# Expert slots of two sizes in a two-layer attention and mixture-of-experts kernel

## The chip, the core and the metric

The kernel runs on one core of one Trainium2 chip. The metric is the device time of one launch in microseconds (us), here the median of several runs. Everything is in fp32.

## What is computed

The input is x of shape (8, 256, 32, 32): 8 batches of 1024 tokens with 256 channels. The reference, cut to what matters:

```
x = attention(x, w_qkv, w_out) + x          # layer 0: 8 heads of 64, softmax over the queries
t = tokens(x)                               # (8, 1024, 256)
n = layer_norm(t)
t = t + softmax((n @ W.T) @ n.T) @ n        # layer 1: one head of 256
n = layer_norm(t)
probs = softmax(n @ router_w.T)             # 8 experts
rw, re = top_k(probs, 2); rw = rw / sum(rw) # two experts for each token
t = t + n + sum over e of combine[:, e] * (gelu(n @ w1[e] + b1[e]) @ w2[e] + b2[e])
```

Every expert has two 256 x 256 matrices. A token goes to 2 of the 8 experts, so batches 0 to 6, with 7168 tokens, give 14336 rows of expert work.

## The kernel before

The batches go one after the other through layer 0 (`layer0`), the attention of layer 1 (`attend`) and the router. The experts of batches 0 to 6 are not computed in their own batch. Each batch's normalized tokens are scattered by `dispatch` into a table in HBM, `rows`: expert e owns the rows from e x 7168 on, its tokens stand there in order, and each row carries two more numbers, the gate and the place of its result. The table is zeroed at the start; past an expert's last row there are zeros. In batch 7 the experts of the seven batches are run over the table as one stage, between the output projection of layer 0 (line 734) and the attention of layer 1. The experts of batch 7 itself come at the end, over all tokens (`dense`), and there the results of the stage are added to batches 0 to 6 (`Results`).

The stage works in slots. A slot is 256 rows (`BR`) of one expert. The number of slots is fixed when the kernel is built: 14336 / 256 + 7 = 63, enough for any split of the rows over 8 experts. Which rows and which weights a slot takes is worked out on the chip by `plan`, a generator on VectorE that is advanced three times during layer 0 of batch 7, beside the projections of head pairs (`project_pair`, line 402): its first half counts blocks for each expert and puts them in an order in which experts of the lower and the upper half alternate; its second half turns each slot's block into a first row and offsets of weights and biases (`row_at`, `w_at`, `b1_at`, `b2_at`). Slots without a block point at zero rows beyond the table, whose targets are out of bounds, so nothing is written for them.

For slot b the function `experts` does:
- `fetch`: four DMAs on the SP queue bring the rows as four squares of channels into `xr` (4 buffers), a fifth the gates and targets into `where`
- `stage`: ScalarE copies the slot's weights into `w_ring` (4 buffers, line 1348)
- `turned`: VectorE transposes `xr` into `xb` (line 1375)
- `hidden`: 4 matmuls `ph` (line 1386, weights stationary, the slot's rows as columns), then 2 gelus on ScalarE (line 1398)
- `collect`: for each 128 rows 2 matmuls `pe` with 256 columns (line 1415), then VectorE adds the bias into `yb` (2 buffers, line 1425)
- `send`: VectorE scales by the gate (line 1440) and forms the targets (line 1443), and GpSimd scatters each 128 rows into `y` in HBM with an indirect DMA (line 1447)

The loop runs these over different slots at once: in one turn `hidden` of b-3, `stage` of b-1, `fetch` of b, `turned` of b-2, `collect` of b-4. An `issue_after` puts an instruction behind another on its queue without a wait. Into turns of the loop small steps of batch 7's layer norm are put. The last four slots (`LATE`) are finished inside the attention of layer 1 of batch 7, as filling.

Of the kernel before, what the change touches and what calls it, by code (L numbers as in the profile page):

```python
# [10 lines left out]
F32 = mybir.dt.float32  # L11
I32 = mybir.dt.int32
# [7 lines left out]
def kernel(  # L20
# [45 lines left out]
    RUN = BR // SQ  # L66
# [96 lines left out]
    for e in range(E):  # L163
# [10 lines left out]
    )  # L174
    HALVES = (NBMAX + 1) // 2
    half_iota = const.tile([P, HALVES, 2], F32, name="half_iota")
    nc.gpsimd.iota(
        half_iota,
        [[1, HALVES], [0, 2]],
        base=0,  # L180
        channel_multiplier=0,
        allow_small_or_imprecise_dtypes=True,
    )
    odd_iota = const.tile([P, HALVES, 2], F32, name="odd_iota")
    nc.gpsimd.iota(
        odd_iota,
        [[0, HALVES], [1, 2]],
        base=0,
        channel_multiplier=0,
        allow_small_or_imprecise_dtypes=True,  # L190
# [885 lines left out]
    class Group:  # L1076


        def __init__(self, n, items):
            self.n, self.items = n, items  # L1080
            self.cap = len(items) * S
            self.nb = 2 * self.cap // BR + E - 1
            self.rows = dram.tile([E * self.cap + BR, DW], F32, name=f"rows_{n}")
            self.views = dram_disjoint_views(self.rows, 2 * NT * len(items))
            self.sums = [dram.tile([P, NT, D], F32, name=f"sums_{b}") for b in items]
            self.y = dram.tile([2 * self.cap, D], F32, name=f"y_{n}")
            self.ways = dram_disjoint_views(self.y, R * self.nb)
            self.counts = None
            self.planes = self.y.rearrange("(k n p i) d -> n p k i d", k=2, p=P, i=NT)
# [118 lines left out]
    def plan(group):  # L1208


        n, nb, cap = group.n, group.nb, group.cap
        counts = group.counts
        steps = cap // BR

        def tmp(tag, shape, dtype=F32):
            return small.tile([P, *shape], dtype, tag=tag, name=f"{tag}_{n}", bufs=1)


        below = tmp("p_below", [E, steps])
        edge = tmp("p_edge", [steps])  # L1220
        nc.vector.tensor_scalar_mul(edge, b_iota[:, :steps], float(BR))
        nc.vector.tensor_tensor(
            below,
            counts.unsqueeze(2).to_broadcast([P, E, steps]),
            edge.unsqueeze(1).to_broadcast([P, E, steps]),
            ALU.is_gt,
        )
        blocks = tmp("p_blocks", [E])
        nc.vector.tensor_reduce(blocks, below, AX.X, ALU.add)
        ends = tmp("p_ends", [E])  # L1230
        nc.vector.tensor_tensor_scan(ends, ones[:, :E], blocks, 0.0, ALU.mult, ALU.add)
        first = tmp("p_first", [E])
        nc.vector.tensor_sub(first, ends, blocks)

        left = ends[:, E // 2 - 1 : E // 2]
        right = tmp("p_right", [1])
        nc.vector.tensor_sub(right, ends[:, E - 1 : E], left)
        turns = tmp("p_turns", [1])
        nc.vector.tensor_tensor(turns, left, right, ALU.min)
        rest = tmp("p_rest", [1])  # L1240
        nc.vector.tensor_tensor(rest, right, left, ALU.is_gt)
        nc.vector.tensor_mul(rest, rest, left)
        nc.vector.tensor_sub(rest, rest, turns)
        twice = tmp("p_twice", [1])
        nc.vector.tensor_add(twice, turns, turns)
        block = tmp("p_block", [nb])
        after = tmp("p_after", [nb])
        taking = tmp("p_taking", [nb])
        half = half_iota.rearrange("p h t -> p (h t)")[:, :nb]
        odd = odd_iota.rearrange("p h t -> p (h t)")[:, :nb]  # L1250
        nc.vector.scalar_tensor_tensor(block, odd, left, half, ALU.mult, ALU.add)
        nc.vector.tensor_scalar_add(after, b_iota[:, :nb], rest)
        nc.vector.tensor_scalar(taking, b_iota[:, :nb], twice, None, ALU.is_lt)
        nc.vector.tensor_sub(block, block, after)
        nc.vector.tensor_mul(block, block, taking)
        nc.vector.tensor_add(block, block, after)
        unused = tmp("p_unused", [nb])
        nc.vector.tensor_scalar(
            unused, b_iota[:, :nb], ends[:, E - 1 : E], float(nb), ALU.is_ge, ALU.mult
        )  # L1260
        nc.vector.tensor_add(block, block, unused)
        base = tmp("p_base", [E])
        nc.vector.tensor_scalar_mul(base, first, -float(BR))
        yield

        mine = tmp("p_mine", [nb, E])
        of = block.unsqueeze(2).to_broadcast([P, nb, E])
        nc.vector.tensor_tensor(
            mine, of, ends.unsqueeze(1).to_broadcast([P, nb, E]), ALU.is_ge
        )  # L1270
        e_of = tmp("p_e", [nb])
        nc.vector.tensor_reduce(e_of, mine, AX.X, ALU.add)
        nc.vector.tensor_tensor(
            mine,
            e_of.unsqueeze(2).to_broadcast([P, nb, E]),
            e_iota.unsqueeze(1).to_broadcast([P, nb, E]),
            ALU.is_equal,
        )

        work = tmp("p_work", [nb, E])  # L1280
        lo, hi = tmp("p_lo", [nb]), tmp("p_hi", [nb])
        nc.vector.tensor_mul(work, mine, base.unsqueeze(1).to_broadcast([P, nb, E]))
        nc.vector.tensor_reduce(lo, work, AX.X, ALU.add)
        nc.vector.scalar_tensor_tensor(lo, block, float(BR), lo, ALU.mult, ALU.add)
        nc.vector.scalar_tensor_tensor(lo, e_of, E - 0.5, lo, ALU.is_lt, ALU.mult)
        nc.vector.scalar_tensor_tensor(lo, e_of, float(cap), lo, ALU.mult, ALU.add)
        nc.vector.tensor_scalar_min(e_of, e_of, float(E - 1))
        row_at = keep.tile([P, NBMAX], I32, tag="row_at", name=f"row_at_{n}", bufs=1)
        placed = nc.vector.tensor_copy(row_at[:, :nb], lo)
        where = [row_at]  # L1290
        for what, each in (("w", WE), ("b1", NFC), ("b2", D)):
            nc.vector.tensor_scalar_mul(hi, e_of, float(each))
            at = keep.tile([P, NBMAX], I32, tag=f"{what}_at", name=f"{what}_at_{n}", bufs=1)
            with tc.issue_after(placed.ins):
                placed = nc.vector.tensor_copy(at[:, :nb], hi)
            where.append(at)
        group.where = where
        yield placed

    def experts(group, behind, table, steps):  # L1300
# [55 lines left out]
        def fetch(b):  # L1356
            xr = rowp.tile([P, RUN, DQ], F32, tag="xr", name=f"xr_{n}_{b}")
            with tc.issue_after((loads[-1] if loads else evicted["relayed"]).ins):
                at = register(b, 0)
            mine = group.rows[bass.ds(at, BR), :D].rearrange("(s t) (k d) -> k t s d", s=RUN, k=NQ)  # L1360
            for k in range(NQ):
                loads.append(nc.sync.dma_start(xr[ts(k, SQ)], mine[k]))
            where = small.tile([P, R, 2], F32, tag="where", name=f"where_{n}_{b}", bufs=8)
            loads.append(
                nc.sync.dma_start(
                    where, group.rows[bass.ds(at, BR), D:].rearrange("(r p) c -> p r c", r=R)
# [5 lines left out]
        def turned(b, xr):  # L1372
            xb = two.tile([P, NCC, BR], F32, tag="xb", name=f"xb_{n}_{b}")
            with tc.issue_after(behind.ins):
                squares = nc.vector.transpose(  # L1375
                    xb.rearrange("p cc (s t) -> p s cc t", t=SQ),
                    xr.rearrange("p s (cc c) -> p s cc c", c=SQ),
                )
            return xb, squares

        def hidden(b, xb):
            wb = firsts.pop(b)
            ph = big(f"ph_{n}_{b}")
            for fc in range(NFC):
                for dc in range(NCC):
                    last = nc.tensor.matmul(  # L1386
                        ph[:, ts(fc, BR)],
# [6 lines left out]
            hT = two.tile([P, NFC, BR], F32, tag=f"qk{1 if late else b % 2}", name=f"hb_{n}_{b}")  # L1394
            at = register(b, 2)
            for fc in range(NFC):
# [3 lines left out]
                        ph[:, ts(fc, BR)],  # L1400
# [7 lines left out]
        def collect(b, hT, last, squares):  # L1408
            wb = seconds.pop(b)
            py = acc(f"pe_{n}_{b}")  # L1410
            at = NCC * FF
            with tc.issue_after(last.ins) if last else nullcontext():
                for r in range(R):
# [8 lines left out]
            yb = two.tile([P, R, D], F32, tag="yb", name=f"yb_{n}_{b}")  # L1422

            def add():
                return nc.vector.tensor_add(
                    yb,
                    py.rearrange("p (r d) -> p r d", d=D),
                    b2_flat[:, bass.ds(register(b, 3), D)].unsqueeze(1).to_broadcast([P, R, D]),
# [8 lines left out]
        def send(b, yb):  # L1437
            if True:
                where = wheres.pop(b)
                scaled = nc.vector.tensor_mul(yb, yb, where[:, :, 0:1].to_broadcast([P, R, D]))  # L1440
                evicted["scaled"] = scaled
                to = small.tile([P, R], I32, tag="to", name=f"to_{n}_{b}", bufs=4)
                nc.vector.tensor_scalar(
                    to, where[:, :, 1], -1.0, float(2 * group.cap), ALU.mult, ALU.add
                )
            for r in range(R):
                sent = nc.gpsimd.indirect_dma_start(  # L1447
                    out=group.ways[R * b + r][:, :],
# [329 lines left out]
```

## Time and profile before

| | us |
|---|---|
| median of 3 runs | 2275.53 |
| lowest and highest run | 2273.93 and 2275.75 |
| profiled execution, its own time | 2280.71 |
| its span, first to last instruction | 2279.0 |
| first `ph` matmul of the expert stage | at 1857.8 |
| last `ph` matmul of the loop | at 2066.3 |

The profile is of one execution on the chip. Times of rows are from the start of its span. An engine's row in the timeline reads: start, duration, engine, line, operation, output and inputs, number of instructions, and in brackets the idle time before it and what ended it. PE is TensorE's matmuls, PEld its weight loads, DVE VectorE, ACT ScalarE, POOL GpSimd, SPq the DMA queue of SyncE. One fp32 matmul shows as two records, each with a weight load.

### The profile page before, as it was taken

What the parts mean: (1) busy time and instruction counts of PE and PEld (TensorE: products, weight loads), DVE (VectorE), ACT (ScalarE), POOL (GpSimd) and SP (SyncE); (2) the same over time, 40 slices, a digit from 0 to 9 for tenths busy, and PEclk for the clock granted to TensorE, in tenths of its full rate; (3) what the DMA queues carried; (4) which work ended last, traced back from release to release, by engine and by line L of the source; (5) the groups of instructions that cost most, each with busy time, mean ns of one, the idle gap of its engine ahead of it and who ended that gap; (6) DMA issues with size and microseconds to landing.
All of it is one profiled execution on the core that took longest, in us unless ns stands there. A gap on an engine that the chain in (4) does not pass through costs nothing.

```text
span 2279.0 us, 38069 instructions
## 1 busy us (share of the span) xinstructions
PE 2239.6 (98%) x13061; PEld 1209.0 (53%) x13061; DVE 1567.8 (69%) x3923; ACT 1232.1 (54%) x2221; POOL 316.3 (14%) x321
## 2 busy tenths in 40 slices
PE   9999999999999999999999999999999999999998
PEld 3345534563356335643555345534563378885666
DVE  5775678567865787577756775678567957555667
ACT  3664566356636564746564664566356645555411
POOL 1000012000300030002000120012000315552100
PEclk9999999999999999999999999999999999999999
DMA  8996201020102010201011000200041136662486
GB/s 281 359 354 191 52 15 43 4 60 8 50 1 46 19 52 6 39 26 45 13 22 43 31 27 13 52 15 25 5 90 51 51 71 150 146 146 53 124 259 170
DMA packets 278265, 182.82 MB, mean 80 GB/s; under 512 B 196676, under 2 KB 233335, under 8 KB 277048
## 3 DMA queue, kind: packets, MB, share of 16 engines
q1 hardware_dynamic: 264808, 150.08, 24.5%
q0 software_dynamic: 11632, 29.78, 3.7%
q8 instruction: 104, 1.70, 0.3%
q14 instruction: 89, 0.73, 0.1%
q10 hardware_dynamic: 1632, 0.52, 0.1%
HBM read 63.47 MB, written 106.61 MB: 75 GB/s over the span
## 4 chain that ended last, share of the span: by engine, by line
PE 85%; issue 4%; ACT 4%; DVE 3%; SPq 2%; DMA 1%; POOL 0%; DVEq 0%; POOLq 0%; ACTq 0%
PE po L626 20%; PE psc L549 20%; PE pqk L402 7%; PE py L943 6%; PE pr L734 5%; PE ph L1386 4%; PE pe L1415 4%; PE pv L432 4%; PE ps L837 3%; PE pdy L1635 2%; PE pdh L1611 2%; PE px L774 2%; PE pqk L380 2%; SPq L926 2%; PE ps1z L837 1%
## 5 line engine op out<-in xcount | busy, mean ns | idle before, releaser
L590 ACT ACTIVATE ex<-psc,nmax 128x1024 f32<-128x1024 f32 x512 | 570.0, 1114 | 295.1 <-DVE scrap L573 212.5
L626 PE MATMUL po<-ex,vs 64*64 64x512 f32 x4096 | 568.7, 591 | 5.3 <-DVE vs L606 4.3
L549 PE MATMUL psc<-qk,qk 64*64 64x512 f32 x4096 | 566.5, 592 | 0.9 <-ACT ex L590 0.8
L573 DVE TENSOR_SCALAR_CACHE_REDUCE scrap<-psc,nmax 128x512 f32<-128x512 f32 x512 | 384.3, 751 | 158.0 <-PE psc L549 129.7
L564 DVE TENSOR_REDUCE nmax<-psc 128x1 f32<-128x512 f32 x512 | 350.5, 685 | 10.7 <-PE psc L549 10.7
L626 PEld LDWEIGHTS po<-ex,vs 64*64 64x64 f32 x4096 | 173.3, 132 | 282.8 <-DVE vs L606 87.3
L549 PEld LDWEIGHTS psc<-qk,qk 64*64 64x64 f32 x4096 | 178.6, 132 | 271.2 <-ACT ex L590 125.0
L1199 POOL DMA_INDIRECT rows<-n,d_at x112 | 109.2, 975 | 463.4 <-DVE nmax L564 425.0
L402 PE MATMUL pqk<-xT,wqkv 128*128 128x512 f32 x384 | 171.2, 599 | 0.0
L1447 POOL DMA_INDIRECT y<-yb,to x126 | 124.5, 988 | 209.7 <-DVE yb L1440 183.6
L367 ACT ACTIVATE qk<-pqk,b_qks 128x512 f32<-128x512 f32 x124 | 85.5, 690 | 88.9 <-PE pqk L402 79.8
L402 PEld LDWEIGHTS pqk<-xT,wqkv 128*128 128x128 f32 x384 | 71.0, 190 | 99.9 <-issue 77.3
L926 ACT COPY spare<-home 32x256 f32<-32x256 f32 x272 | 109.4, 402 | 17.4 <-DVE home L914 11.9
L432 PE MATMUL pv<-wqkv,xT 128*128 128x512 f32 x244 | 116.4, 600 | 1.0 <-DVE v L454 1.0
L1386 PE MATMUL ph<-xb,w_ring 128*128 128x256 f32 x488 | 115.2, 379 | 1.3 <-DVE xb L1375 1.3
L1191 POOL IOTA n<- 128x8 f32 x14 | 2.0, 145 | 820.5 <-PE py L943 820.5
L943 PE MATMUL py<-n,spare 128*128 128x256 f32 x512 | 114.9, 379 | 0.0
L734 PE MATMUL pr<-wo,res 128*128 128x256 f32 x512 | 111.9, 379 | 0.7 <-ACT res L645 0.7
L1415 PE MATMUL pe<-w_ring,hb 128*128 128x256 f32 x472 | 111.5, 379 | 0.0
L1398 ACT ACTIVATE hb<-ph,b1T 128x256 f32<-128x256 f32 x126 | 52.7, 470 | 108.6 <-PE ph L1386 105.6
L943 PEld LDWEIGHTS py<-n,spare 128*128 128x128 f32 x512 | 96.5, 190 | 20.1 <-issue 4.3
L734 PEld LDWEIGHTS pr<-wo,res 128*128 128x128 f32 x512 | 97.2, 190 | 17.8 <-ACT res L645 4.7
(265 smaller groups left out, 2842.8 us busy)
## 6 DMA issues: line engine op xcount, KB each, us to landing
rows<-zero SPq DMA_DIRECT2D x7, 8256.0 KB
xr<-rows SPq DMA_DIRECT2D x252, 64.0 KB
xs<-in_x_dram SPq DMA_DIRECT2D x64, 128.0 KB
ys<-y SPq DMA_DIRECT2D x16, 512.0 KB
spare<-home SPq DMA_DIRECT2D x240, 32.0 KB
out_dram<-oT SPq DMA_DIRECT2D x58, 128.0 KB
xT<-in_x_dram SPq DMA_DIRECT2D x7, 1024.0 KB
sums<-t SPq DMA_DIRECT2D x7, 1024.0 KB
```

Of the source, the lines that this page charges most:

```text
L402: mm = nc.tensor.matmul(pq[:, ts(n, 512)], wqkv[:, cc, t, ts(g, P)], xT[:, cc, ts(n, 512)], start=(cc == 0), stop=(cc == NCC - 1),)
L432: return nc.tensor.matmul(pv, self.xT[:, cc, ts(i, P)], wqkv[:, cc, 2, :], start=(cc == 0), stop=(cc == NCC - 1),)
L549: mm = nc.tensor.matmul(pss[at, h][ts(c, DK), ts(n, 512)], k[r, j * P + c * DK : j * P + (c + 1) * DK], q[r, ts(n, 512)], start=True, stop ...
L564: firsts[at, h] = nc.vector.tensor_reduce(nmax, pss[at, h][:, ts(0, 512)], AX.X, ALU.max, negate=True)
L573: seconds[h] = nc.vector.tensor_scalar(scrap, pss[at, h][:, ts(1, 512)], -1.0, nmaxes[at, h], ALU.mult, ALU.min, accum_out=nmax,)
L590: nc.scalar.activation(ex, pss.pop((at, h)), AF.Exp, bias=nmaxes.pop((at, h)), scale=1.0, accum_out=sums[at][:, h : h + 1],)
L626: mm = nc.tensor.matmul(po[n][ts(h, DK), :], vss[at][keys, h, :], exps[at, h][keys, ts(n, 512)], start=(j == 0 and turn == 0), stop=(j == ...
L734: nc.tensor.matmul(pr[:, :C], res[g][:, ts(i, P)], wo[:, g, :], start=(g == 0), stop=(g == NPAIR - 1))
L926: move(to[ts(k, SQ), a], since[ts(a, SQ), k])
L943: evicted["mixed"] = nc.tensor.matmul(py[:, :D], aT[m], n1[:, m, :], start=(m == 0), stop=(m == NT - 1))
L1386: last = nc.tensor.matmul(ph[:, ts(fc, BR)], wb[:, dc * FF + fc * P : dc * FF + (fc + 1) * P], xb[:, dc, :], start=(dc == 0), stop=(dc == ...
L1415: mm = nc.tensor.matmul(py[:, ts(r, D)], hT[:, fc, ts(r, P)], wb[:, ts(fc, D)], start=(fc == 0), stop=(fc == NFC - 1),)
```

## The change

The 63 slots get two sizes: 56 slots of 256 rows and 7 of 128. The 7 small ones stand spread among the others, at positions 4, 13, 22, 31, 40, 49 and 58. An expert's rows are cut into whole blocks of 256; if at most 128 rows are left over, they go into a slot of their own. A left-over of more than 128 rows counts as a whole block. Whole blocks take the large slots first; the left-overs take the large slots that remain and then the small ones. If there are more whole blocks than large slots, a whole block goes into two small ones. The experts follow each other in plain order; the alternation of the two halves of the experts is gone. `plan` is rewritten for this, all functions of the slot take their size from `group.size[b]`, and a new constant, `virtual`, holds for each position its place in the order of large and then small slots. The two constants `half_iota` and `odd_iota` go.

```diff
@@ class Group
-            self.nb = 2 * self.cap // BR + E - 1
+            self.full = 2 * self.cap // BR
+            self.half = E - 1
+            self.nb = self.full + self.half
+            halves = [(2 * j + 1) * self.nb // (2 * self.half) for j in range(self.half)]
+            fulls = [p for p in range(self.nb) if p not in halves]
+            self.order = [0] * self.nb
+            for k, p in enumerate(fulls + halves):
+                self.order[p] = k
+            self.size = [P if p in halves else BR for p in range(self.nb)]
+            self.virtual = const.tile([P, self.nb], F32, name=f"virtual_{n}")
...
+                nc.gpsimd.iota(
+                    self.virtual[:, at:end],
...
@@ def plan, first half
-        steps = cap // BR
+        steps = cap // P
...
-        blocks = tmp("p_blocks", [E])
-        nc.vector.tensor_reduce(blocks, below, AX.X, ALU.add)
+        units = tmp("p_units", [E])
+        nc.vector.tensor_reduce(units, below, AX.X, ALU.add)
+        fulls = tmp("p_fulls", [E])
+        nc.vector.tensor_reduce(
+            fulls, below.rearrange("p e (s t) -> p e s t", t=2)[:, :, :, 1], AX.X, ALU.add
+        )
+        halves = tmp("p_halves", [E])
+        nc.vector.scalar_tensor_tensor(halves, fulls, -2.0, units, ALU.mult, ALU.add)
...
-        block = tmp("p_block", [nb])
...
-        nc.vector.tensor_add(block, block, unused)
...
+        nc.vector.tensor_tensor(
+            mine,
+            unit.unsqueeze(2).to_broadcast([P, nb, E]),
+            twice.unsqueeze(1).to_broadcast([P, nb, E]),
+            ALU.is_ge,
+        )
+        nc.vector.tensor_reduce(e_of, mine, AX.X, ALU.add)
         yield
@@ def plan, second half
+        odd_e = tmp("p_odd_e", [nb])
         nc.vector.tensor_tensor(
-            mine, of, ends.unsqueeze(1).to_broadcast([P, nb, E]), ALU.is_ge
+            mine,
+            odd.unsqueeze(2).to_broadcast([P, nb, E]),
+            odds.unsqueeze(1).to_broadcast([P, nb, E]),
+            ALU.is_ge,
         )
-        nc.vector.tensor_reduce(e_of, mine, AX.X, ALU.add)
+        nc.vector.tensor_reduce(odd_e, mine, AX.X, ALU.add)
+        nc.vector.tensor_sub(e_of, e_of, odd_e)
+        nc.vector.tensor_mul(e_of, e_of, whole)
+        nc.vector.tensor_add(e_of, e_of, odd_e)
...
-        nc.vector.tensor_mul(work, mine, base.unsqueeze(1).to_broadcast([P, nb, E]))
+        nc.vector.tensor_mul(work, mine, ends.unsqueeze(1).to_broadcast([P, nb, E]))
         nc.vector.tensor_reduce(lo, work, AX.X, ALU.add)
-        nc.vector.scalar_tensor_tensor(lo, block, float(BR), lo, ALU.mult, ALU.add)
-        nc.vector.scalar_tensor_tensor(lo, e_of, E - 0.5, lo, ALU.is_lt, ALU.mult)
+        nc.vector.tensor_mul(work, mine, fulls.unsqueeze(1).to_broadcast([P, nb, E]))
+        nc.vector.tensor_reduce(hi, work, AX.X, ALU.add)
+        nc.vector.scalar_tensor_tensor(lo, lo, -2.0, unit, ALU.mult, ALU.add)
+        nc.vector.tensor_mul(lo, lo, whole)
+        nc.vector.scalar_tensor_tensor(lo, hi, 2.0, lo, ALU.mult, ALU.add)
+        nc.vector.tensor_scalar_mul(lo, lo, float(P))
@@ def experts (br = group.size[b], rs = br // P)
-            xr = rowp.tile([P, RUN, DQ], F32, tag="xr", name=f"xr_{n}_{b}")
+            xr = rowp.tile([P, run, DQ], F32, tag="xr", name=f"xr_{n}_{b}")
...
-                        ph[:, ts(fc, BR)],
+                        ph[:, ts(fc, br)],
...
-                for r in range(R):
+                for r in range(rs):
                     for fc in range(NFC):
                         mm = nc.tensor.matmul(
...
-            for r in range(R):
+            for r in range(rs):
                 sent = nc.gpsimd.indirect_dma_start(
```

## The prediction

> **What bounds the kernel now.** I read the page first (shares, slices), then the busy time in windows of the expert stage, then the timeline of one slot in it, then the timeline around the plan in batch 7 beside the same place in batch 6.
>
> ```profile
> PE 2239.6 (98%) x13061; PEld 1209.0 (53%) x13061; DVE 1567.8 (69%) x3923; ACT 1232.1 (54%) x2221; POOL 316.3 (14%) x321
> ...
> PEclk9999999999999999999999999999999999999999
> ```
>
> TensorE is busy for 98% at full granted clock, so the question is whether its work gets shorter where it is gapless. A busy PE row is modelled, so the stage is checked by starts. The window from 1857 to 2052 us is the expert stage:
>
> ```profile
> 1857.00:2052.00 195.00, 195.00 (x905) 171.67 (x904) 119.41 (x245) 102.49 (x172) 106.55 (x108) 1.00 0.62 145
> ```
>
> PE fills all 195 us; VectorE 61%, ScalarE 53%, GpSimd 55%, DMA 62%. One slot on the timeline:
>
> ```profile
> 1945.90 1.89 PE L1386 MATMUL ph<-xb,w_ring 128*128 128x256 f32 x8
> 1946.11 0.69 DVE L1425 TENSOR_TENSOR yb<-pe,b_all 128x512 f32<-128x512 f32 x1 [1.42 <-PE pe L1415]
> 1946.71 0.16 DVE L1443 TENSOR_SCALAR to<-where 128x2 int32<-128x2 f32 x1
> 1946.83 0.69 DVE L1440 TENSOR_TENSOR yb<-yb,where 128x512 f32<-128x512 f32 x1
> 1947.44 0.70 DVE L1375 STREAM_TRANSPOSE xb<-xr 128x512 f32<-128x512 f32 x1
> 1947.63 1.89 PE L1415 MATMUL pe<-w_ring,hb 128*128 128x256 f32 x8
> 1949.09 0.98 POOL L1447 DMA_INDIRECT y<-yb,to  x1 [0.30 <-issue]
> 1949.36 1.89 PE L1386 MATMUL ph<-xb,w_ring 128*128 128x256 f32 x8
> ```
>
> Starts, not durations, give the rate: first products (8 records, two per fp32 matmul) at 1945.90, second at 1947.63, the next slot's at 1949.36. So a slot costs 1.73 + 1.73 = 3.45 us, 0.216 us per 256-column record. VectorE waits 1.42 us in each slot for PE. The stage is bound by PE alone; a shorter slot shortens the kernel as long as the others keep up.
>
> The plan is the other place the change touches. VectorE is nearly full in the attention of layer 0. Batch 6 (no plan) and batch 7 (second half of the plan before the transposes of L501):
>
> ```profile
> 1539.30 7.13 PE L402 MATMUL pqk<-xT,wqkv 128*128 128x512 f32 x16
> 1547.53 0.75 DVE L573 TENSOR_SCALAR_CACHE_REDUCE scrap<-psc,nmax 128x512 f32<-128x512 f32 x1 [4.93 <-PE psc L549]
> ...
> 1780.45 7.13 PE L402 MATMUL pqk<-xT,wqkv 128*128 128x512 f32 x16
> 1787.29 2.37 DVE L501 STREAM_TRANSPOSE t<-xs 128x1024 f32<-128x1024 f32 x2
> 1789.59 0.71 DVE L573 TENSOR_SCALAR_CACHE_REDUCE scrap<-psc,nmax 128x512 f32<-128x512 f32 x1
> ```
>
> Behind the same projection, VectorE waits 4.93 us in batch 6. In batch 7 it has no idle left and takes up the scores 1789.59 - 1780.45 = 9.14 us after the projection's start instead of 8.23: 0.91 us late. PE paid: its L626 group at 1562.73 in batch 6 stands at 1804.57 in batch 7, 241.84 apart, where the projections are 241.15 apart. So an overrun of 0.91 us cost PE 0.69: about 0.2 is covered, what goes beyond is paid in full.
>
> **The change part by part.**
>
> *Seven slots of 128 rows.* They stand at positions 4, 13, 22, 31, 40, 49, 58, all before the last four, so nothing moves in the code that fills the last attention. What PE issues is static: it does not depend on the tokens. In a half slot the second products fall from 4 matmuls to 2: 4 records less, 4 x 0.216 = 0.86 us. The first products stay 4 matmuls (8 records) with 128 columns instead of 256. What does a record of 128 columns cost behind its own 128x128 fp32 weight load? The nearest row is the count matmul of the router with 64 columns and the same load:
>
> ```profile
> 1482.94 0.19 PEld L1137 LDWEIGHTS pqk<-d_both,before 128*128 128x128 f32 x1 [0.24 <-issue]
> 1483.37 0.19 PEld L1137 LDWEIGHTS pqk<-d_both,before 128*128 128x128 f32 x1 [0.24 <-issue]
> 1483.48 0.19 PEld L1137 LDWEIGHTS pqk<-d_both,ones 128*128 128x128 f32 x1
> 1483.59 0.19 PEld L1137 LDWEIGHTS pqk<-d_both,ones 128*128 128x128 f32 x1
> ```
>
> Loads start every 0.11 us although each is shown as 0.19, and the matmuls between follow at that pace, where 64 columns alone would be a quarter of 0.216. So loads run at 0.11 us, overlapped with the matmul before. 128 columns are half of 0.216, 0.108: the two just match, and a record costs 0.11. Bounds: 0.108 (columns alone) and 0.19 (no overlap of loads, as their shown length). First products: 8 x (0.216 - 0.11) = 0.85 us saved.
> A rule speaks against that: the Trainium skill, "TensorE: Matmul & The Clock Gate", section "Back-to-back issue gap", says that in a stream of load and matmul pairs the spacing is set by both, about 81 ns at 128 columns where a lone matmul would take about 56. In that ratio a record would cost 0.108 x 81/56 = 0.156 us and the first products save 0.48. By the row seven slots save 7 x (0.86 + 0.85) = **12.0 us**, by the rule 7 x (0.86 + 0.48) = 9.4 us. I take the row (same load, same kernel) and keep the rule for a rival.
>
> *What must keep up around a half slot.* Count from the end of the second products before it (slot h-2). PE then does the short first products 0.88 and the full second products of h-1, 1.73, and asks for slot h+1's transpose at 2.61 us. VectorE adds, forms the targets, scales (1946.11 to 1947.44: 1.33, begun 0.2 late), transposes 0.70: ready at 2.23. Cover 0.38 us where a full slot has 1.2. The norm steps of batch 7 (0.42 + 0.18 statistics, 0.41 write) still ride on slots 4 to 22 and break it: 0.2 us late near slot 13, 0.06 twice near slot 22. I book **0.5 us** of stalls, bounds 0 and 1.5. Half-size VectorE and ScalarE work in those slots (L737 shows 0.42 for 256 elements against 0.69) only adds cover. Weight copies are ahead by two slots. SP's five issues take 2.6 us per slot (1848 to 1853, unhindered), as long as the shortened slot; the four row buffers keep it three transposes (about 9 us) ahead, so nothing is paid; without that cover it would be at most 7 x 0.1 us.
>
> *GpSimd scatters.* One instead of two in a half slot. But yb has two buffers: the add of slot s waits for the scatter of s-2. In the steady slot the second scatter issues at 1949.09 and the add two slots on comes at 1953.01, so landing has 3.9 us; in 3 of 60 slots landing did end that wait. Around a half slot the two slots last 5.2 instead of 6.9 us, so it has 2.2. The add then waits up to 1.7 us; behind it on VectorE stand the scale and the transpose of h+3, PE asks for that at 8.65 us, and late by 1.7 it is ready at 8.66. Nothing reaches PE.
>
> *The plan.* First half (beside the projection at 1745.76): two 504-element operations move here (0.6 us pitch each among independent neighbours), the comparison grows from 224 to 448 elements (+0.23), so does its reduction, a second reduction (0.3) comes; sixteen operations of 1 to 63 elements go and seven come (0.07 to 0.25 each). Net about +0.9 us. VectorE waits 2.04 us there for the scores (1751.94 to 1753.98): hidden. Without that cover it would cost 0.9.
> Second half (1781.38 to 1787.29, no cover left): before, five 504-element operations and three on 63. After, seven of the first and eight of the second kind, some between independent ones. Pitch of a 504-element operation 0.71, of a dependent 63-element one 0.26, of an independent one 0.13 to 0.15: 4.3 us become 6.7, **+2.4 us**, bounds 1.6 (all overlapped) and 2.9 (none). By the batch 6/7 comparison it is past the covered 0.2 us, so PE pays it whole. Queued behind it are the transposes of L501 and the maxima; exponentials and gathers wait for those. The scheduler also swaps two score groups on PE there; I book nothing.
>
> *Rest.* 15 small iotas replace two long ones on GpSimd: at most 15 x 0.2 - 0.95 = 2 us; GpSimd is idle from 7.15 us until the first relays past 34 us: nothing. The last slot holds real rows where it was empty; the adds of the results start at 2164.02, 5 us after their loads land at 2158.6, and ScalarE, not the scatter, releases the last stage: nothing. Plain order of experts moves no instruction.
>
> Sum: -12.0 + 2.4 + 0.5 = **-9.1 us**. The durations are from one execution of 2280.7 us (span 2279.0 and 1.7 around it), 5.2 us over the median of the runs, 2275.5. It holds one PE stall of 1.3 us near 2054 behind a late scatter that other runs may not have. The difference is taken off the median: **2266.4 us**.
>
> **The rivals.**
> - *The load binds at 128 columns* (the rule): 9.4 - 2.9 = 6.5 us gained, 2269.0. Against it stands 0.11 us at 64 columns.
> - *PE absorbs the longer plan*, the maxima catching up or the swapped order helping: -11.5, 2264.0. Against it: 0.69 of 0.91 was paid.
> - *Half slots break the rhythm*: transposes or late scatters cost 0.7 us or more at each, 7 x 0.7 = 5 or more, gain 4 or less, 2271.5 to 2276. For it: cover 0.38 us. Against: VectorE's own work halves there.
> - *Slower: the scatter's landing becomes the cycle.* In plain order neighbouring slots belong to one expert, so their reads lie close and their scatters go to one stretch of tokens. If landing is longer for that, the two yb buffers decide from 3.9 us on: each further 1 us costs 0.5 us per slot, 28 us over 56. The gain is gone at 3.9 + 9.1/28 = 4.2 us; at 4.5, +8 us, 2283. For it: landing already ended the wait 3 times in 60. Against: the byte count falls and targets are still spread over 14336 rows.
> - *It does not do what it says*: excluded for PE's work, which is static.
>
> **How the numbers follow.** Main case 0.60, load binds 0.12, plan absorbed 0.12, broken rhythm 0.10, slower by landing 0.06. 0.2% is 4.6 us, about what a measurement of this kernel can tell from no change. Main, load and plan cases are faster by more (0.84), of the broken rhythm 0.03 too; 0.07 within; 0.06 slower. Range 2262.0 to 2272.0: unknown costs of main (2264 to 2268), both fast rivals, 2 us of stray, and the better part of the broken rhythm.
>
> **What would show it.** The 128-column records of ph start every 0.11 us and such a slot takes 1.74 us of PE; the stretch from the first ph to the last falls by about 11.5 us. VectorE takes up the scores about 11.5 us after the projection at 1780 and PE's next groups stand about 2.4 us later against batch 6 than now. Wrong would be: records at 0.15 or more, PE idle behind xb in each half slot, yb waits for y at more than a few slots, or plan time not seen on PE.

## The result, and the profile after

| | before | after |
|---|---|---|
| median of the runs, us | 2277.23 (16 runs, 2273.93 to 2279.55) | 2271.78 (16 runs, 2268.57 to 2275.35) |
| profiled execution, its own time | 2280.71 | 2274.83 |
| its span | 2279.0 | 2273.1 |

The ratio after to before is 0.9977, 95% interval 0.9969 to 0.9985: the change takes off 5.5 us, where 9.1 had been forecast. A second comparison of the same two kernels gave 0.9968 [0.9958, 0.9978]. So it is faster, as forecast, but by 5.5 to 7.3 us (the two medians). On the median that the forecast started from, 2275.53 x 0.9977 = 2270.3 us, near the upper end of the range and 3.9 us above the number.

To see where the time went, four marks on TensorE are enough: the first `pr` matmul (output projection of layer 0) of batch 6 and of batch 7, the first `px` (attention of layer 1, behind the expert stage), and the first `pdy` (experts of batch 7).

| stretch, us | before | after | difference |
|---|---|---|---|
| pr of batch 6 to pr of batch 7 (holds the plan) | 241.36 | 245.39 | +4.0 |
| pr of batch 7 to px (the expert stage) | 225.08 | 217.41 | -7.7 |
| px to pdy | 90.32 | 86.87 | -3.5 |
| pdy to the end | 119.63 | 120.88 | +1.2 |

The last two rows are not the change's work. In the twelve traces taken later, px to pdy is 86.9 or 90.3 us (once 88.6) and pdy to the end 119.3 to 119.6 or 120.8 to 120.9, in kernels with and without half slots alike. The longer px to pdy goes with a lower clock: before has 0.91 from 2140 to 2160 us, after 1.00. So the question is the first two rows: the plan was to cost 2.4, the stage to give back 11.5.

The busy row and the clock row of the page look as before, and so does the window over the stage (columns: busy us and instructions of PE, PEld, DVE, ACT, POOL, then clock, DMA share, GB/s). A slice of the clock row is 57 us long, so a low clock of a few us does not show in it:

```profile
PE 2231.4 (98%) x13033; PEld 1200.3 (53%) x13033; DVE 1567.1 (69%) x3924; ACT 1231.3 (54%) x2221; POOL 309.7 (14%) x327
...
PEclk9999999999999999999999999999999999999999
```

```profile
1861.00:2052.00 191.00, 190.65 (x906) 167.26 (x905) 119.32 (x255) 104.00 (x177) 102.86 (x105) 1.00 0.62 145
```

TensorE is still full. The first half slot on the timeline of after:

```profile
1873.96 1.05 PE L1406 MATMUL ph<-xb,w_ring 128*128 128x128 f32 x8
...
1874.85 1.89 PE L1435 MATMUL pe<-w_ring,hb 128*128 128x256 f32 x8
...
1876.58 1.89 PE L1406 MATMUL ph<-xb,w_ring 128*128 128x256 f32 x8
...
1878.31 1.03 PE L1435 MATMUL pe<-w_ring,hb 128*128 128x256 f32 x4
...
1879.17 1.89 PE L1406 MATMUL ph<-xb,w_ring 128*128 128x256 f32 x8
...
1880.20 0.43 DVE L1445 TENSOR_TENSOR yb<-pe,b_all 128x256 f32<-128x256 f32 x1 [1.38 <-DMA y<-yb,to]
```

By starts, the eight 128-column records take 1874.85 - 1873.96 = 0.89 us and the four second products 1879.17 - 1878.31 = 0.86 us: 1.75 us for the slot instead of 3.45. Seven of them save 11.9 us. The last line is new: the half slot's add waits 1.38 us for a scatter into y. In after such waits stand in ten places (three in before): at the half slots 4, 13, 22, 31, 40 and 49, at the slots 23, 25 and 32 shortly behind one, and at slot 57.

The plan, after. VectorE's own lateness is as forecast: scores taken up 1791.94 - 1780.48 = 11.46 us after the projection.

```profile
1789.64 2.37 DVE L483 STREAM_TRANSPOSE t<-xs 128x1024 f32<-128x1024 f32 x2
1791.94 0.71 DVE L555 TENSOR_SCALAR_CACHE_REDUCE scrap<-psc,nmax 128x512 f32<-128x512 f32 x1
...
1796.07 0.75 DVE L555 TENSOR_SCALAR_CACHE_REDUCE scrap<-psc,nmax 128x512 f32<-128x512 f32 x1 [0.92 <-PE psc L531]
```

```profile
1780.48 7.13 PE L384 MATMUL pqk<-xT,wqkv 128*128 128x512 f32 x16
...
1794.01 1.99 PE L531 MATMUL psc<-qk,qk 64*64 64x512 f32 x8 [2.81 <-ACT ex L572]
1795.78 1.85 PE L608 MATMUL po<-ex,vs 64*64 64x512 f32 x8
1797.45 1.03 PE L531 MATMUL psc<-qk,qk 64*64 64x512 f32 x8
```

TensorE waits 2.81 us, and then two groups of eight take 1.77 and 1.67 us from start to start instead of 0.86. Behind the late VectorE there is a TensorE that has become slow, and VectorE waits for it in turn (0.92 us at 1796.07). The window over those four microseconds gives a granted clock of 0.57:

```profile
1793.50:1797.50 4.00, 3.49 (x20) 1.10 (x24) 2.98 (x8) 2.25 (x5) 2.72 (x2) 0.57 0.02 4
```

The end of the stage has a second such place. Just ahead of the half slot at position 58 the scatters of slot 55 come behind a pause on GpSimd, and the add of slot 57 waits for them:

```profile
2051.44 0.98 POOL L1466 DMA_INDIRECT y<-yb,to  x1 [2.65 <-issue]
2052.72 1.28 POOL L1466 DMA_INDIRECT y<-yb,to  x1 [0.30 <-issue]
...
2057.26 0.69 DVE L1445 TENSOR_TENSOR yb<-pe,b_all 128x512 f32<-128x512 f32 x1 [3.49 <-DMA y<-yb,to]
...
2058.59 0.70 DVE L1395 STREAM_TRANSPOSE xb<-xr 128x512 f32<-128x512 f32 x1
...
2059.44 2.98 PE L1406 MATMUL ph<-xb,w_ring 128*128 128x256 f32 x8 [2.55 <-DVE xb L1395]
```

Read it as a chain: the scatter is issued late, lands late, the add that reuses its buffer waits, the transpose stands behind the add, and TensorE waits for the transpose. The second products at 2055.87 need 0.86 us and the next group starts at 2059.44, so 2.7 us are lost, and again the groups behind it are slow (2.77 us for `ph` instead of 1.73, 3.16 for the transposes `pt_n` instead of 2.45).

In before the same pause stands ahead of full slots, and 1.3 us are lost behind it:

```profile
2045.96 0.98 POOL L1447 DMA_INDIRECT y<-yb,to  x1 [2.65 <-issue]
```

```profile
2054.40 1.97 PE L1386 MATMUL ph<-xb,w_ring 128*128 128x256 f32 x8 [1.28 <-DVE xb L1375]
```

### The profile page after: what moved, and what is told of

Same layout as the page of the kernel before. It is cut to its first block, busy times and chain, and to the rows that moved or that the text cites. A ratio compares the mean times of both kernels' runs of the same rounds, so it can differ in the third digit from the quotient of the medians.

```text
span 2273.1 us, 38013 instructions
## 1 busy us (share of the span) xinstructions
PE 2231.4 (98%) x13033; PEld 1200.3 (53%) x13033; DVE 1567.1 (69%) x3924; ACT 1231.3 (54%) x2221; POOL 309.7 (14%) x327
## 4 chain that ended last, share of the span: by engine, by line
PE 80%; issue 5%; ACT 4%; DVE 4%; SPq 2%; POOL 2%; DMA 1%; POOLq 0%; DVEq 0%; ACTq 0%
PE po L608 20%; PE psc L531 20%; PE pqk L384 7%; PE py L925 7%; PE pr L716 5%; PE pv L414 4%; PE ps L819 3%; PE px L756 2%; POOL y L1466 2%; SPq L908 2%; PE pdh L1630 2%; PE pdy L1654 2%; PE pqk L362 2%; PE ps1z L819 2%; PE ph L1406 1%
## 5 line engine op out<-in xcount | busy, mean ns | idle before, releaser
L546 DVE TENSOR_REDUCE nmax<-psc 128x1 f32<-128x512 f32 x512 | 350.8, 685 | 10.7 <-PE psc L531 10.7
L1466 POOL DMA_INDIRECT y<-yb,to x119 | 117.4, 986 | 209.2 <-DVE yb L1459 185.6
L908 ACT COPY spare<-home 32x256 f32<-32x256 f32 x272 | 109.4, 402 | 17.3 <-DVE home L896 11.9
L1406 PE MATMUL ph<-xb,w_ring 128*128 128x256 f32 (+1 forms) x488 | 110.7, 370 | 2.9 <-DVE xb L1395 2.8
L1418 ACT ACTIVATE hb<-ph,b1T 128x256 f32<-128x256 f32 (+1 forms) x126 | 51.3, 459 | 101.1 <-PE ph L1406 101.1
L1435 PE MATMUL pe<-w_ring,hb 128*128 128x256 f32 x444 | 105.5, 379 | 0.0
```

The lines of the kernel that those rows point to most:

```text
L546: firsts[at, h] = nc.vector.tensor_reduce(nmax, pss[at, h][:, ts(0, 512)], AX.X, ALU.max, negate=True)
L908: move(to[ts(k, SQ), a], since[ts(a, SQ), k])
L1406: last = nc.tensor.matmul(ph[:, ts(fc, br)], wb[:, dc * FF + fc * P : dc * FF + (fc + 1) * P], xb[:, dc, :], start=(dc == 0), stop=(dc == ...
L1466: sent = nc.gpsimd.indirect_dma_start(out=group.ways[sum(group.size[:b]) // P + r][:, :], out_offset=bass.IndirectOffsetOnAxis(ap=to[:, r ...
```

## The experiments

All in the table were compared with the kernel before on the same chip (e11_bplan6 and e12_bplan9, below, ran once each and have no ratio); "idle" is TensorE's wait behind the plan in batch 7, "clock" the granted clock from 1793.5 to 1797.5 us.

| kernel | ratio to before [95%] | pr to pr | pr to px | idle | clock |
|---|---|---|---|---|---|
| after | 0.9977 [0.9969, 0.9985] | 245.39 | 217.41 | 2.81 | 0.57 |
| after, second comparison (e8_again) | 0.9968 [0.9958, 0.9978] | 245.42 | 217.44 | 2.80 | 0.62 |
| e1_order | 0.9967 [0.9956, 0.9978] | 245.42 | 214.26 | 1.95 | 0.58 |
| e2_move | 0.9955 [0.9942, 0.9968] | 241.44 | 214.13 | 0.44 | 1.00 |
| e3_yb3 | 0.9966 [0.9953, 0.9978] | 243.69 | 214.74 | 2.81 | 1.00 |
| e4_bplan | 1.0012 [1.0006, 1.0018] | 243.23 | 223.73 | 2.24 | 1.00 |
| e5_place | 0.9984 [0.9976, 0.9991] | 245.56 | 216.65 | 2.80 | 0.69 |
| e6_no58 | 0.9970 [0.9960, 0.9980] | 243.89 | 212.91 | 2.80 | 1.00 |
| e7_best | 0.9965 [0.9954, 0.9976] | 241.39 | 215.67 | 0.44 | 1.00 |
| e9_best2 | 0.9953 [0.9939, 0.9967] | 241.36 | 213.31 | 0.44 | 1.00 |
| e10_pause | 0.9965 [0.9953, 0.9976] | 243.79 | 215.15 | 2.80 | 1.00 |

e4_bplan is the kernel before with full slots only, and its trace has no TensorE stall in the stage, so 223.73 is what the stage of before takes undisturbed; the trace of before has one stall of 1.3 us in it.

**Is the swapped order of the score groups the price? (e1_order)**

```
+            swap = b == B - 1 and (g, j) in ((2, 3), (2, 4))
+            if swap:
+                score(at - 1, 1, 1)
             if at <= last:
                 with ...:
                     score(at, 0, 0)
             if 1 < at <= last + 1:
-                with ...:
-                    score(at - 1, 1, 1)
+                if not swap:
+                    with ...:
+                        score(at - 1, 1, 1)
```

> The changed kernel, with one thing undone: in batch 7, at the two steps behind the projection of the last head pair (2,3 and 2,4), TensorE takes the second half of the old score tile before the first half of the new one, as it did in the kernel before. Theory (the swap of the score groups is a cost of its own, about 1.7 us of the 4.0 that the plan cost): the output projection of batch 7 (pr) starts about 1846.3 instead of 1847.96, the idle of 2.81 us on TensorE behind the projection becomes about 1 us, ratio to the kernel before about 0.9970 instead of 0.9977. Rival (all of it is VectorE's lateness, the order only shows where it is waited for): pr stays within 0.3 us of 1848 and the ratio at 0.9977.

The theory fell. pr to pr is 245.42, the same as in after; TensorE does four records earlier and then waits all the same, and its clock is as low. The ratio of 0.9967 cannot be told from after's. That the prediction booked nothing for the swap was right.

**Is VectorE's lateness the price? (e2_move)**

```
-                    with tc.issue_after(ahead.ins):
-                        t1, parts = residual(b, xs)
+                    if b < B - 1:
+                        with tc.issue_after(ahead.ins):
+                            t1, parts = residual(b, xs)
                 if g == 0:
+                    if b == B - 1:
+                        with tc.issue_after(firsts[at, 1].ins):
+                            t1, parts = residual(b, xs)
```

> The changed kernel with VectorE's two residual transposes of batch 7 (2.37 us behind the plan's second half) moved two head pairs earlier, beside the first projection, where VectorE waits 5.4 us. TensorE's order stays that of the changed kernel. Theory (the plan's overrun on VectorE is what TensorE pays, and the order costs only when VectorE is late): scores taken up about 9.1 us after the projection instead of 11.46, pr near 1844 instead of 1848, ratio about 0.9960. Rival (the swapped order costs by itself, whatever VectorE does): pr not before 1845.5, ratio 0.9967 or more.

```profile
1790.15 1.04 PE L608 MATMUL po<-ex,vs 64*64 64x512 f32 x8
1791.63 1.09 PE L531 MATMUL psc<-qk,qk 64*64 64x512 f32 x8 [0.44 <-ACT ex L572]
1792.54 1.04 PE L608 MATMUL po<-ex,vs 64*64 64x512 f32 x8
```

TensorE's wait falls from 2.81 to 0.44 us, the groups behind it take 0.9 us, and pr to pr is 241.44: all 4.0 us are back, with the order of after kept. So the 2.3 us by which VectorE is later cost TensorE 4.0 us in after, wait and slow groups together.

**Do the late scatters need a third buffer? (e3_yb3)**

```
-            yb = two.tile([P, rs, D], F32, tag="yb", name=f"yb_{n}_{b}")
+            yb = two.tile([P, rs, D], F32, tag="yb", name=f"yb_{n}_{b}", bufs=3)
...                                              # the plan's work arrays share a buffer
```

> The changed kernel with three result buffers (yb) instead of two; to make room two work arrays of the plan share one buffer. The add of a slot then waits for the scatter of three slots before. Theory (late scatters around half slots reach TensorE): VectorE's waits of yb for y fall from 16.4 us in 10 places to under 2, the stretch from pr to px falls from 217.4 to about 214, ratio about 0.9964. Rival (these waits have cover; the 2.7 us stall near 2056 was one late scatter of one execution): ratio stays within 0.0004 of 0.9977, stretch falls by less than 1.5 us or only by the stall at the end.

The profile shows no add that waits for y any more. The stalls at slots 13 (0.48 us), 22 (0.17) and 49 (0.32) are as large as with two buffers, so the waits of the adds there have cover, as the prediction had it. At slot 58 a stall of 0.5 us is left where e1_order and e2_move show 1.3; but then TensorE waits 2.08 us for px instead of 0.54, for a cause that stays open, and pr to px is no shorter. The edit gave an answer on the plan, too: the same wait of 2.81 us, but with full clock behind it, and pr to pr is 243.69 instead of 245.4.

```profile
1793.77 1.09 PE L531 MATMUL psc<-qk,qk 64*64 64x512 f32 x8 [2.81 <-ACT ex L572]
1794.68 1.04 PE L608 MATMUL po<-ex,vs 64*64 64x512 f32 x8
1795.54 1.04 PE L531 MATMUL psc<-qk,qk 64*64 64x512 f32 x8
```

Against the lines of after: 0.91 and 0.86 us from start to start where after has 1.77 and 1.67. The longer plan without the low clock costs 243.69 - 241.36 = 2.3 us; the other 1.7 are the clock.

**The longer plan alone (e4_bplan, e11_bplan6, e12_bplan9)**

```
         nc.vector.tensor_tensor(mine, of, ends..., ALU.is_ge)
         e_of = tmp("p_e", [nb])
+        for _ in range(3):                      # 6 and 9 in the other two
+            nc.vector.tensor_scalar_min(mine, mine, 2.0)
         nc.vector.tensor_reduce(e_of, mine, AX.X, ALU.add)
+        nc.vector.tensor_scalar_min(e_of, e_of, 99.0)
```

> The kernel before with four more operations in the plan's second half that change no value (three on 504 elements, one on 63, each needing the one before it): 3 x 0.71 + 0.26 = 2.4 us on VectorE. With it TensorE's program has the two score groups in the order of the changed kernel. Theory (2.4 us of overrun cost 4.0 us with that order): pr of batch 7 4.0 us later than in the kernel before, ratio 1.0018. Rival (TensorE pays just the overrun): 2.4 us later, 1.0011. Third (part of the overrun is absorbed): under 2 us, 1.0008 or less.

pr to pr is 243.23, 1.9 us more than in before, ratio 1.0012 [1.0006, 1.0018]. VectorE was 1.75 us later here than in before (scores taken up 1791.53 - 1780.64 = 10.89 us after the projection instead of 9.14), not 2.4 as estimated: the three added operations ran 0.5 us each. The wait was 2.24 us, the clock stayed at 1.00, and TensorE paid about the lateness, as the rival had it. The other two made the wait longer.

> The kernel before with seven more operations in the plan's second half that change no value: 1.5 us more than the run with four. TensorE's idle behind the plan was 2.24 us there with full clock after it, and should be about 3.7 us here. Theory (a long idle brings half clock for some 3.4 us, at a price of 1.7 us, surely if it is longer than 3.4, as the Trainium skill has it in 'TensorE: Matmul & The Clock Gate', Part 1; by luck of the phase if it is shorter): pr to pr 243.2 + 1.5 + 1.7 = 246.4, clock about 0.5 for 3.4 us after the idle. Rival (the dip has another cause than the idle): 244.7, clock 1.00.

> The same with ten more operations, 3.0 us more than the run with four: idle about 5.2 us. Theory: pr to pr 243.2 + 3.0 + 1.7 = 247.9, the dip as long as with the shorter idle, so it is a fixed price. Rival (the dip grows with the idle, or there is none): over 249, or 246.2.

```profile
1796.86 1.99 PE L549 MATMUL psc<-qk,qk 64*64 64x512 f32 x8 [3.23 <-ACT ex L590]
1798.62 1.62 PE L626 MATMUL po<-ex,vs 64*64 64x512 f32 x8
```

```profile
1796.19 1.99 PE L549 MATMUL psc<-qk,qk 64*64 64x512 f32 x8 [4.99 <-ACT ex L590]
1797.95 1.93 PE L626 MATMUL po<-ex,vs 64*64 64x512 f32 x8
1799.65 1.47 PE L549 MATMUL psc<-qk,qk 64*64 64x512 f32 x8
```

The first fence is e11_bplan6, the second e12_bplan9. Waits of 3.23 and 4.99 us are both followed by slow groups; pr to pr is 246.18 and 248.03 (246.4 and 247.9 expected by the theory, 244.7 and 246.2 by the rival). But the dip is no fixed price: the clock stood at 0.50 for 3.41 us in e11 and for 6.83 us in e12, and from the end of the wait to pr TensorE took 53.71 and 54.40 us, where e4 took 52.27. So the slow groups cost 1.4 and 2.1 us, and the theory's 247.9 for e12 came true by luck.

Why the same wait of 2.8 us brings a dip in three traces (after twice, e5_place) and none in three others (e3_yb3, e6_no58, e10_pause) can be read from the moments at which the clock changes. In each of the fourteen traces they lie whole multiples of 3.413 us apart, so the clock is set in windows of that length. Their phase differs from one execution to the next: the first change comes 4.4 to 7.5 us after the start. Here are the window with the wait and the next one, first in after and then in e3_yb3 (first number behind the length: us in which TensorE is busy; 1.00 and 0.50 are the clock):

```profile
1790.60:1794.01 3.41, 0.61 (x8) 0.00 (x0) 3.29 (x6) 1.21 (x2) 0.00 (x0) 1.00 0.00 0
1794.01:1797.42 3.41, 3.41 (x16) 1.05 (x20) 2.46 (x8) 1.71 (x3) 2.64 (x2) 0.50 0.02 5
```

```profile
1788.52:1791.93 3.41, 2.44 (x24) 0.61 (x16) 3.29 (x7) 0.00 (x0) 0.00 (x0) 1.00 0.00 0
1791.93:1795.35 3.42, 1.58 (x16) 0.75 (x20) 3.14 (x9) 2.41 (x4) 0.97 (x1) 1.00 0.02 5
1795.35:1798.76 3.41, 3.41 (x36) 1.25 (x34) 3.03 (x9) 2.41 (x4) 3.23 (x3) 1.00 0.09 31
```

In after the wait falls into one window and TensorE is busy for only 0.61 us of it; in e3_yb3 a boundary splits the same wait. All ten traces with a wait of 1.95 us or more here follow this: behind windows with 0.61 to 1.48 us of TensorE work the clock is 0.50 (after, e8_again, e1_order, e5_place, e11, and in e12 twice in a row), behind those with 1.58 us or more it is 1.00 (e3_yb3, e6_no58, e10_pause, e4_bplan). So e4 escaped by the phase, too (2.23 and 2.35 us), and its 2.24 us are no safe length. This bound is for this place: near 2165 us a window with only 1.2 us of idle was followed by half clock (e4_bplan).

**Other places for the half slots (e5_place, e6_no58)**

```
-            halves = [(2 * j + 1) * self.nb // (2 * self.half) for j in range(self.half)]
+            halves = [25, 29, 33, 37, 41, 45, 49]        # e5_place
+            halves = [4, 13, 22, 27, 31, 40, 49]         # e6_no58
```

> The changed kernel with the seven half slots at positions 25, 29, 33, 37, 41, 45 and 49, so that none shares its turns with the norm steps of batch 7 (slots 0 to 22) and none lies behind the place where GpSimd pauses 2.65 us in all six traces so far (before the scatter with index 104 into y, which is its 217th indirect DMA). Theory (the stalls of 0.47 and 0.16 us at slots 13 and 22 come from the norm steps, the 1.3 us at slot 58 from the pause, each meeting the thin cover of a half slot): the stretch from pr to px falls from 214.2 us (without the longer stall of the first trace) to about 212.1, nothing over 0.3 us is left, the pause is still before scatter index 104; ratio about 0.0009 under the changed kernel's, 0.9968. Rival (the thin cover alone stalls, wherever a half slot stands): 214 or more, stalls at most of the new positions.

Not faster than after: 0.9984, against 0.9977 and 0.9968. The stalls at 13 and 22 did go, so they belong to the norm steps. But one of 1.2 us came behind the pause although only full slots stand there, and new ones of up to 1.2 us came behind the later of the half slots that follow each other at four slots' distance. The trace shows a queue there that the theory left out. From the waits between 1850 and 2064 us (engine, line, what for: total us, times, longest):

```profile
DVE xb L1395 <- DMA xr<-rows: 5.8, 4, 1.8
PE ph L1406 <- DVE xb L1395: 3.0, 4, 1.0
```

```profile
2015.97 0.71 DVE L1395 STREAM_TRANSPOSE xb<-xr 128x512 f32<-128x512 f32 x1 [1.59 <-DMA xr<-rows]
...
2016.83 1.97 PE L1406 MATMUL ph<-xb,w_ring 128*128 128x256 f32 x8 [0.28 <-DVE xb L1395]
```

VectorE waits for row loads, which it does nowhere in after. A half slot needs as many loads as a full one (four of rows, one of gates), in half of TensorE's time. The waits begin only at slot 48, behind the sixth half slot, and e6_no58 below has none with half slots at 22, 27 and 31. That fits a lead of the four row buffers that shrinks with each half slot in a row and is refilled at nine slots' distance; no run varied the number of buffers, so this reading is argued, not shown.

> The changed kernel with only the last half slot moved, from position 58 to 27. Theory (pause behind scatter index 104 meets the half slot at 58): the stall there goes, pr to px falls from 214.2 to about 212.9, the stalls at 13, 22 and 49 stay as they are; ratio about 0.9971. Rival (it is the end of the loop, with the first copies into w_late, that stalls): pr to px stays at 214, the stall of 1.3 us stands near slot 58 with a full slot there.

As the theory has it: pr to px 212.91, no stall from slot 50 on, the others where they were. The pause is still there; here TensorE, with a full slot behind it, does not see it:

```profile
2049.56 0.98 POOL L1466 DMA_INDIRECT y<-yb,to  x1 [2.10 <-issue]
```

```profile
2053.21 1.89 PE L1435 MATMUL pe<-w_ring,hb 128*128 128x256 f32 x8
2054.94 1.92 PE L1406 MATMUL ph<-xb,w_ring 128*128 128x256 f32 x8
```

The timed gain against after (0.9970) is too small to be told apart; the trace carries this point. It is one execution, and the other traces show that the full slot is only half of it. The add behind the pause was let go either 1.6 to 2.2 us or 3.3 to 4.0 us after its scatter's issue had ended. With full slots there TensorE lost nothing in the short case (e4, e6, e9, e11) and 1.1 to 1.8 us in the long one (before, e5, e7, e12); with the half slot at 58 it lost 1.3 us in the short case (e1, e2) and 2.7 or more in the long one (after twice). So the half slot adds about 1.3 us, and the length of the landing the rest.

**What the pause is tied to (e10_pause).** Its edit issues four of the scatters of batch 0's tokens twice:

```
+                if which == 0 and k == 0 and i < 4:
+                    scatter = nc.gpsimd.indirect_dma_start(...)   # the same again
```

> The changed kernel with four of GpSimd's indirect DMAs of batch 0 issued twice (same rows to the same places), so that four more stand ahead of the expert stage. Nothing in the stage itself is edited. Theory (the pause of 2.65 us comes with the 217th indirect DMA, whatever it is): the pause stands before the scatter with index 100 into y instead of 104, two slots earlier and clear of the half slot at 58; the stall there falls under 0.3 us and pr to px from 214.2 or more to about 212.9. Rival (the pause belongs to a place of the program or to the time): still before index 104, stall of 1.1 us or more.

```profile
2043.25 0.98 POOL L1473 DMA_INDIRECT y<-yb,to  x1 [2.48 <-issue]
```

The pause moved to index 100, so it is tied to the count: in all fourteen traces GpSimd pauses 2.1 to 2.7 us before its 217th indirect DMA. What it does there the traces do not show. The other half of the theory failed: the stall at 58 fell only to 1.0 us, and 0.8 us came at a full slot near 2050, where the add waited 3.53 us for its scatter, a long landing. Moving the pause two slots did not give what moving the half slot gave in e6_no58.

**Together (e7_best, e9_best2)**

> The changed kernel with both remedies: the residual transposes of batch 7 beside the first projection, and the half slots at 25 to 49. If the two are independent: plan costs nothing against the kernel before (pr to pr 241.4), pr to px about 212.1, together 223.7 - 212.1 = 11.6 us less than the kernel before, ratio about 0.9949. Rival (the end of the stage is then held by something else, such as the residual sums on GpSimd or SP's loads): 0.9955 or more, as with the move alone.

> The changed kernel with the two single remedies that worked: the residual transposes of batch 7 beside the first projection, and the last half slot moved from 58 to 27. If they add up: pr to pr 241.4, pr to px 212.9, together 13.1 us less than the 245.4 + 214.2 of the changed kernel's usual shape with the dip, 10.8 us less than the kernel before; ratio about 0.9950. Rival (one undoes the other, as with the half slots close together): 0.9960 or more.

e7_best joins e2_move and the close half slots of e5_place. It cannot be told from after: the plan's 4.0 us are back, but VectorE waits for row loads again, and 1.8 us are lost behind the pause. e9_best2 joins e2_move and e6_no58: pr to pr 241.36, pr to px 213.31, 10.4 us less than the undisturbed before, and a ratio of 0.9953 [0.9939, 0.9967], 10.7 us. Its ratio is the lowest of all kernels here, and its interval lies below that of after's first comparison; it cannot be told from the second one, nor from e2_move alone (0.9955).

**The same kernel again (e8_again)**

> The changed kernel itself, a second profile. Theory (TensorE's idle of 2.81 us behind the plan is sometimes followed by some 3.4 us at half clock, by the phase of whatever sets the clock, and sometimes not): pr to pr is either about 243.7, with clock 1.00 from 1793 to 1798, or about 245.4 with 0.5 to 0.65 there; the stall at slot 58 is 1.3 us, not 2.7, since two other kernels with the same slots showed 1.28 and 1.26. Rival (both are fixed properties of this program): 245.4 and 2.7 us again. Ratio 0.9970 to 0.9980.

The rival's numbers came: the low clock (0.62) is back, and at slot 58 2.9 us are lost. That does not make the dip a fixed property of the program. The windows of the clock happened to lie alike in the two executions (first change at 5.42 and 5.89 us), while the kernels with the same wait and no dip had them at 6.76 to 7.50. The long landing at slot 58 came in both traces of after and in neither of e1_order and e2_move, which have the same slots; why stays open.

## Why the prediction was off, step by step

- *Records of 128 columns at 0.11 us*: right, 0.89 us for eight. The Trainium skill's rule for streams of loads and matmuls ("TensorE: Matmul & The Clock Gate", "Back-to-back issue gap"), scaled as in the prediction, would have given an estimated 1.25; the measurement decides. Half slots save the 12.0 us that were booked.
- *Plan, first half hidden*: right. VectorE's wait for the scores fell from 2.04 to 1.11 us, and TensorE pays nothing there.
- *Plan, second half, +2.4 us, "so PE pays it whole"*: this step failed. The lateness was 2.32 us and costs 2.3 (e3_yb3), but in both traces of after the term is 4.0. What was missing is TensorE's clock: behind the wait of 2.8 us it stood at half for 3.41 us, which is 1.7 us of lost work. The same page of the Trainium skill, Part 1, says that the clock falls after an idle window of about 3.4 us and that the window runs free. The traces agree on the free-running window of 3.41 us, but it need not be idle to the end: up to 1.48 us of work in it did not keep the clock up. So a wait shorter than the window is enough when the phase is bad. The prediction read the full clock row of a gapless kernel and did not ask what its own stall would do to it.
- *Stalls around half slots, "I book **0.5 us**", bounds 0 and 1.5*: this step failed too. Without slot 58 they are 1.0 to 1.2 us (0.47 at 13, 0.16 at 22, the rest mostly at 40 and 49), with it 2.4 in e2_move, and in after 5.7: 0.47, 0.16, 0.31 and 0.27, then 2.7 at slot 58 and 1.0 and 0.7 in the slow groups behind it. 12.0 - 5.7 is the 6.3 us between 223.73 and 217.41.
- *Scatters, "Nothing reaches PE"*: right for the ordinary half slot to within 0.3 us (at 40 in after, behind a wait of 2.36 us); wrong for the one behind the pause. The late scatter near 2054 stood in the trace of before, and the prediction put it down to chance ("other runs may not have"). Half of that was right: the pause comes before the same 217th indirect DMA in every trace, but with full slots behind it TensorE stalled in four traces of eight.
- *The swap booked at nothing*: right (e1_order). *The tail, POOL's iotas*: no loss shows there. *Slower by landing in plain order*: did not happen, half slots apart the steady slots keep 3.45 us.

So the forecast of 9.1 becomes 12.0 - 2.3 - 1.0 - 1.3 = 7.4 us in an execution without dips and with the shorter stall at 58, and 12.0 - 4.0 - 5.7 = 2.3 us in one like the two traces of after. The two medians, 5.5 and 7.3, lie between. The clock of the timed runs says how much of this is dips: it is 0.9970 and 0.9971 in the mean of the two sets of after (25 runs) and 0.9976 to 0.9978 in the three sets of before (77 runs). Over the span that is 6.6 to 6.8 us of clock missing, against 5.0 to 5.5. So the dips that the change brought cost about 1.4 us in an average execution, an estimate, as the clock of a run is recorded to three digits. With it 7.4 becomes about 6 us.

## What to carry to other kernels

A stall on a full TensorE can be priced twice: its length, and a clock that may run at half for some microseconds afterwards. Here waits of 2 to 3.2 us cost up to 1.7 us more, or nothing, by where the clock's windows fell; one execution does not tell which. Before a unit of work is shortened, list every engine and queue that does as much for the short one as for the long (here the row loads), and leave them room between short ones to catch up. A stall in the trace of before is to be explained, not put down to chance: if it comes at a fixed count, as this pause does, the change may put its tightest place on top of it.

## What was not expected of the hardware

- GpSimd pauses 2.1 to 2.7 us before its 217th indirect DMA, in each of fourteen traces; four more of them ahead shift it by four.
- The clock changed only in steps of 3.413 us, at a phase that differs from execution to execution, so kernels with the same wait of 2.8 us showed a dip in one trace and none in another.
- The second indirect DMA behind the pause, issued in 1.27 us, let the waiting add go 1.8 us after its end in e1_order and 3.3 us after it in after: 1.3 or 2.7 us on TensorE. What makes that difference stays open.
- The stretch from px to pdy is 86.9 or 90.3 us for the same work, by whether the clock falls in it. That limits what the span of one profile of this kernel can say: compare stretches, and look at their clock first.
